# Moving a kernel's plain loads from SyncE's queue to GpSimd's, with measured durations in its planner

## The chip, the cores and the metric

The kernel runs on one core of a Trainium2 chip. The metric is device time in microseconds (us), the median over executions of the whole program. The core's engines are named as in the profile: PE is TensorE (matmuls; PEld are its weight loads), DVE is VectorE, ACT is ScalarE, POOL is GpSimd, SP is SyncE. SP computes nothing; it issues DMAs.

## What is computed

The reference takes x [2, 1024, 2048], a context [2, 2048, 2048], a weight matrix W [2048, 2048] and eight low-rank expert pairs of rank 16 with a router. Cut to what matters:

```python
def xattn(x1, x2):                       # x1: layernormed x, x2: context
    q1 = (clip(round(x1 / s1 + z1), 0, 255) - z1) * s1
    q2 = (clip(round(x2 / s2 + z2), 0, 255) - z2) * s2
    return matmul(q1, q2)                # [2,1024,2048] x [2,2048,2048]

def ffn(x):                              # x: layernormed again
    w = top2_softmax_weights(x @ W_router.T)          # 8 experts
    h = einsum('td,erd->ter', x, lora_A)
    return x @ W.T + b + 2 * einsum('ter,eor,te->to', h, lora_B, w)

x = x + xattn(layernorm(x), ctx)
x = x + ffn(layernorm(x))
```

The first matmul works on integers after rounding to 8 bits, which fp16 holds exactly. The second keeps about fp32 precision: each operand is split into a high and a low fp16 part, and three products are summed.

## The kernel before

**Work and stages.** Rows are handled in blocks of 128: eight blocks for each of the two batches (`NT`), in four pairs (`NP`). For each batch b there are these stages.

- The x blocks are loaded (`load_x`), their layernorm statistics are made on DVE (`ln1`, `stats`, `rstd_seed`), and the inverse square root is refined by a Newton chain of 16 small operations (`rstd_newton`, L389 to L400, and L582 to L584), on DVE for the very first block, on POOL for all others. ACT then quantizes to 8 bits (q, L346 through the helper `affine`), ACT or DVE shifts to fp16 (qn, L346 or L355), and a DMA transpose on SP (`transpose`, L336) makes the stationary operand `at`.
- The context is loaded in 512 KB pieces (`load_b`, tile `bs`), quantized on DVE (u, L357) and shifted to fp16 on ACT or DVE (b, L346 or L355).
- `gemm1` runs 32 units of 16 matmuls of 128x128 by 128x512 (L636). DVE adds the result into x (L657), ACT sums squares (L675). The very first matmuls are 30 warm-up ones on qn (L609).
- `ln2` makes the second layernorm's scale for a pair of blocks (POOL for three pairs, DVE for the last), and `y_prep` normalizes into yt, forms sums and differences of the row and column halves (a Strassen-like scheme of 7 products instead of 8; L749), splits each into high and low fp16 parts (nat_a, nat_s: L346 and L742) and transposes them by DMA (y_a, y_s; L336). Most halves of x are then written out to DRAM (spill) and later read back (xr, `reload`).
- `w_step` loads rows of W (wt, wb, ws), combines them on DVE (L918, L928, L932, L939, L942), scales to a high part on ACT or DVE (w, L346 or L353) and makes the low part on DVE (L902). `g2` multiplies (L1032; the low-rank part in L1046), in two column halves (`cp`) and four groups (`GROUPS`); DVE adds the result into x (L1057). `hmm` (L790, L794) makes the low-rank and router products, `router` picks two experts. `put` stores the finished blocks (L1002).
- Once only: `prep_lora` and `prep_bmax` find scales of the low-rank matrices, `w_norm` (tile wn) the norm of W. Two of these need a maximum or a sum over the partitions, which POOL makes with `partition_all_reduce` (L491, L537).

The tiles come from pools of fixed slots (48 slots of 4 KB per partition for nearly everything, tag "u"; 8 PSUM banks), so a load can start when an earlier user of its slot is done.

**What sets the order.** All work is first entered as tasks in a planner (`Plan.add`: engine, duration, buffers read and written, due time). Where a task has two engines, its durations are a dictionary and the planner picks. `Plan.rank` works due times back from the matmuls, and `Plan.order` runs a list scheduling in made-up time: each engine takes the ready task with the earliest due time that fits into the free slots; a DMA also has to find the modelled queue less than `DEPTH` = 2.5 us behind and fewer than `LANES` = 8 in flight. What comes out is one order of tasks, which is emitted as it stands. On the chip each engine runs its own part of that order, and each instruction waits for its semaphores, so the planner's times set the order but not when things happen. The lines with the durations of DMAs:

```python
add("SP", 0.47, lambda: nc.sync.dma_start(...), ..., dma=nbytes * P / 360e3)
add("SP", 1.25, lambda: nc.sync.dma_start_transpose(...), ..., dma=0.896 * cols / 1024)
```

All DMAs, that is loads, spills, transposes and stores, are issued by SP in this one order. `load` (L332) issues the loads and, with a DRAM tile as its target, the spills.

Of the kernel before, what the change touches and what calls it, by code (L numbers as in the profile page):

```python
# [11 lines left out]
F32 = mybir.dt.float32  # L12
# [5 lines left out]
ALU = mybir.AluOpType  # L18
AX = mybir.AxisListType
PSUM = bass.MemoryType.PSUM  # L20

P = 128
# [21 lines left out]
MM = 0.216  # L44
# [22 lines left out]
DMA_SLACK = 3.0  # L67

# [14 lines left out]
class Task:  # L83
    __slots__ = ("eng", "dur", "durs", "fn", "preds", "succs", "prio", "cap", "bufs", "left",
                 "ready", "start", "done", "dma", "seq", "pe", "far", "need")


class Plan:
# [3 lines left out]
    def add(self, eng, dur, fn, r=(), w=(), prio=None, cap=None, dma=None, far=None):  # L92
# [7 lines left out]
        t.far = far  # L100
# [40 lines left out]
    def order(self):  # L141
# [6 lines left out]
        dma_free = 0.0  # L148
        lag = 0.0
# [43 lines left out]
        while todo:  # L193
# [8 lines left out]
            for eng in busy:  # L202
                while busy[eng] <= now:
# [35 lines left out]
                    end = now + t.dur  # L239
                    busy[eng] = end  # L240
                    wake(end)
                    if t.dma is not None:
                        dma_free = max(now + 1.1, dma_free) + t.dma
                        t.done = dma_free + 2.0
                        lanes = [x for x in lanes if x > now] + [t.done]
                    else:
                        t.done = end + 0.2
# [22 lines left out]
def xattn_ffn_kernel(ctx, tc, x, cx, scal, wT, bias, arT, bT, out):  # L270
# [41 lines left out]
    nc.gpsimd.memset(magic, 0x5F3759DF)  # L312
    iota = const.tile([P, E], F32)
# [17 lines left out]
    def load(dst, dst_ap, src, nbytes, w, r=(), **kw):  # L331
        add("SP", 0.47, lambda: nc.sync.dma_start(dst_ap(), src() if callable(src) else src),  # L332
            r=r, w=w, dma=nbytes * P / 360e3, **kw)

    def transpose(dst, src, r, w, cols, **kw):
        add("SP", 1.25, lambda: nc.sync.dma_start_transpose(dst(), src()),  # L336
            r=r, w=w, dma=0.896 * cols / 1024, **kw)

    def affine(dst, src, n, r, w, scale=None, bias=None, only=None, **kw):
# [19 lines left out]
        durs = {"ACT": n * 0.00083 + 0.19 + 0.09 * ptrs, "DVE": n * 0.00053 + 0.08 + 0.06 * ptrs}  # L359
# [49 lines left out]
    def prep_lora(when):  # L409
        a32 = []  # L410
        ps = bank("arn")
        on = buf("u", [P, P], F32, "ones")
        add("POOL", 0.2, lambda: nc.gpsimd.memset(on.ap(), 1.0), w=[on])
        for q in range(4):
# [11 lines left out]
            def mm(q=q, s=v):  # L426
                for k in range(4):
                    nc.tensor.matmul(
                        ps.ap()[:, :AR], on.ap(), s.ap()[:, k, :], start=q + k == 0,
# [3 lines left out]
            add("PE", 1.0, mm, r=[v, on], w=[ps], prio=when + q)  # L433
# [35 lines left out]
        for q in range(2):  # L469
# [3 lines left out]
            add("DVE", 0.6,  # L473
# [4 lines left out]
    def prep_bmax():  # L478
        m = buf("sm", [P, 52], F32, "sm_bmax")
        for h in range(2):  # L480
            s = buf("u", [P, HD], F32, f"bms_{h}")
            load(s, s.ap, bT[:, h * HD : (h + 1) * HD], HD * 4, [s])
            add("DVE", 1.13,
# [6 lines left out]
        add("POOL", 1.5,  # L490
            lambda: nc.gpsimd.partition_all_reduce(  # L491
                b_max, m.ap()[:, 2:3], P, bass_isa.ReduceOp.max), r=[m], w=[bmax_b])

        def fin():
            a = m.ap()
            i = a[:, 3:4].bitcast(I32)
# [691 lines left out]
```

## Time and profile before

| | before |
|---|---|
| median of 2 runs | 966.77 us (965.12 and 968.43) |
| span of the profiled execution | 965.8 us |
| PE busy in it | 913.9 us |
| DVE, ACT, POOL busy | 734.1, 379.9, 100.0 us |
| mean granted TensorE clock | 0.989 |
| bytes moved by DMA | 243.12 MB, 252 GB/s on the mean |
| plain loads and spills (L332) | 392 |
| transposes (L336) | 75 |
| stores (L1002) | 36 |

The profiled execution is one execution of the program on the chip; its span runs from its first to its last instruction, and is 1.0 us under the median of the runs. A matmul counts as PE busy; a weight load (PEld) runs beside it. DMA-issuing instructions are not counted as busy: their rows carry the engine's name with a q (SPq), and their length is the time that the issue held that engine. In a timeline each row has start, length, engine, line, operation, out<-in, and in brackets the engine's idle time ahead of it and what ended that. In the list of waits the idle time of an engine is summed by what ended it. The granted clock (PEclk) is given in shares of full speed.

By stages: PE starts with the warm-up at 14.56 us and is full from 41 to 158 us (first matmul of batch 0); the second matmul of batch 0 runs until about 500 us, the first of batch 1 until about 614 us, the second until 962 us.

### The profile page before, as it was taken

Reading aid. Unit: us, or ns where it says so; the run is one execution under the profiler, and the core shown is the slowest. Engines: PE = TensorE matmul, PEld = TensorE weight load, DVE = VectorE, ACT = ScalarE, POOL = GpSimd, SP = SyncE. Lnnn points to the kernel's source line nnn. Section 1 sums busy time; section 2 is a strip of 40 time slices with the busy share of each in tenths; the row PEclk is TensorE's granted clock in tenths of the full one; section 3 lists DMA queues with packets and bytes.
Section 4 is the critical chain, followed back from the end, with each engine's and each line's share of the span. In section 5 each row is a group of like instructions: output and inputs, shape, how many; then the busy total and the mean of one; then the engine's idle time right before and its main releaser. Section 6 shows DMA issues by size and latency. Waiting matters only on the chain.

```text
span 965.8 us, 12426 instructions
## 1 busy us (share of the span) xinstructions
PE 913.9 (95%) x4478; PEld 431.5 (45%) x4478; DVE 734.1 (76%) x1229; ACT 379.9 (39%) x440; POOL 100.0 (10%) x353
## 2 busy tenths in 40 slices
PE   3699998997999999999999999997898999999998
PEld 1245445454444444444444444545543444444443
DVE  7579887996988876999555778987597876699231
ACT  3466785641425422243555644641230321225000
POOL 3405431000000000005220223000000000000000
PEclk9799999999999999999999999999999999999999
DMA  9999999899899986966999979899978479695011
GB/s 319 246 392 336 303 313 243 214 189 233 246 302 389 360 312 244 363 219 242 239 273 356 319 190 228 245 215 185 255 180 262 163 272 325 207 356 171 34 66 66
DMA packets 225518, 243.12 MB, mean 252 GB/s; under 512 B 160944, under 2 KB 162992, under 8 KB 225456
## 3 DMA queue, kind: packets, MB, share of 16 engines
q1 hardware_dynamic: 225456, 242.33, 83.0%
q8 instruction: 35, 0.57, 0.2%
q14 instruction: 27, 0.22, 0.1%
HBM read 172.03 MB, written 31.46 MB: 211 GB/s over the span
## 4 chain that ended last, share of the span: by engine, by line
PE 62%; DVE 19%; POOL 6%; DMA 5%; issue 5%; ACT 2%; SPq 1%; DVEq 0%; POOLq 0%; ACTq 0%
PE X L1032 28%; PE Y L1032 19%; PE g L636 11%; DVE yt_a L749 2%; DVE nat_s L742 2%; DVE w L902 2%; PE X L1046 2%; PE Y L1046 2%; DVE nat_a L742 2%; DMA wb<-in_wT_dram 2%; DVE xr L1057 1%; POOL sm L399 1%; POOL sm L395 1%; DMA wt<-in_wT_dram 1%; DVE x L657 1%
## 5 line engine op out<-in xcount | busy, mean ns | idle before, releaser
L636 PE MATMUL g<-b,at 128*128 128x512 f16 x1024 | 228.5, 386 | 9.2 <-ACT b L346 7.4
L1032 PEld LDWEIGHTS <-y_s 128*128 128x128 f16 x1536 | 149.8, 98 | 192.4 <-issue 9.9
L1032 PE MATMUL Y<-w,y_s 128*128 128x512 f16 x768 | 207.1, 380 | 5.7 <-DVE hf L809 2.8
L1032 PE MATMUL X<-w,y_s 128*128 128x512 f16 x768 | 207.7, 381 | 4.3 <-DVE w L902 2.6
L1032 PE MATMUL X<-w,y_a 128*128 128x512 f16 x768 | 190.4, 380 | 4.5 <-DVE w L902 2.6
L1032 PEld LDWEIGHTS <-y_a 128*128 128x128 f16 x1152 | 112.5, 98 | 144.9 <-issue 7.3
L636 PEld LDWEIGHTS <-at 128*128 128x128 f16 x1024 | 101.4, 99 | 133.6 <-issue 17.5
L346 ACT ACTIVATE w<-wb,gW 128x1024 f16<-128x1024 f32 x59 | 67.4, 1147 | 190.3 <-DVE wb L932 94.3
L1032 PE MATMUL Y<-w,y_a 128*128 128x512 f16 x384 | 103.3, 379 | 3.8 <-DVE xr L1057 2.7
L902 DVE SCALAR_TENSOR_TENSOR w<-wb,gW,w 128x1024 f16<-128x1024 f32 x64 | 81.6, 1278 | 11.7 <-ACT w L346 11.3
L357 DVE TENSOR_SCALAR u<-bs,rec,sc 128x1024 uint8<-128x1024 f32 x64 | 50.9, 808 | 27.5 <-DMA bs<-in_cx_dram 22.0
L346 ACT ACTIVATE b<-u,nz 128x1024 f16<-128x1024 uint8 x47 | 53.0, 1143 | 44.7 <-DVE u L357 40.2
L1057 DVE SCALAR_TENSOR_TENSOR xr<-X,uW,xr 128x512 f32<-128x512 f32 x70 | 50.5, 744 | 25.7 <-PE X L1046 23.2
L1057 DVE SCALAR_TENSOR_TENSOR xr<-Y,uW,xr 128x512 f32<-128x512 f32 x45 | 33.2, 742 | 36.0 <-PE Y L1046 36.0
L657 DVE SCALAR_TENSOR_TENSOR x<-g,s,x 128x512 f32<-128x512 f32 x64 | 47.4, 745 | 10.3 <-PE g L636 10.1
L346 ACT ACTIVATE q<-x,sm 128x1024 uint8<-128x1024 f32 x32 | 38.0, 1232 | 34.0 <-POOL sm L584 29.2
L928 DVE TENSOR_TENSOR wb<-wt 128x512 f32<-128x512 f32 x32 | 21.9, 687 | 34.4 <-DMA wt<-in_wT_dram 28.7
L939 DVE TENSOR_TENSOR wb<-wb,wt 128x1024 f32<-128x1024 f32 x32 | 38.7, 1218 | 11.5 <-DMA wb<-in_wT_dram 11.5
L742 DVE TENSOR_TENSOR nat_s<-yt_a,nat_s 128x1024 f16<-128x1024 f32 x32 | 38.3, 1217 | 5.5 <-ACT nat_s L346 5.5
L367 DVE BATCH_NORM_STATS2 sm<-x 128x6 f32<-128x512 f32 x64 | 40.4, 680 | 2.5 <-DMA x<-in_x_dram 2.4
L346 ACT ACTIVATE nat_s<-yt_a 128x1024 f16<-128x1024 f32 x27 | 27.8, 1049 | 33.3 <-DMA y_s<-nat_s 14.9
L790 PE MATMUL ph<-ar,y_a 128*128 128x272 f16 x192 | 37.0, 284 | 3.9 <-DVE xr L1057 2.1
(157 smaller groups left out, 901.8 us busy)
## 6 DMA issues: line engine op xcount, KB each, us to landing
wt<-in_wT_dram SPq DMA_DIRECT2D x88, 512.0 KB, 6.4
bs<-in_cx_dram SPq DMA_DIRECT2D x64, 512.0 KB, 9.9
wn<-in_wT_dram SPq DMA_DIRECT2D x32, 512.0 KB, 7.6
wb<-in_wT_dram SPq DMA_DIRECT2D x32, 512.0 KB, 8.1
x<-in_x_dram SPq DMA_DIRECT2D x30, 512.0 KB, 8.3
spill<-x SPq DMA_DIRECT2D x28, 512.0 KB, 4.0
xr<-spill SPq DMA_DIRECT2D x28, 512.0 KB, 6.8
out_dram<-xr SPq DMA_DIRECT2D x24, 512.0 KB, 4.2
```

What stands on the lines that cost most here:

```text
L346: nc.scalar.activation(o, i, AF.Copy if c is None else AF.Identity, scale=1.0 if a is None else a, bias=0.0 if c is None else c,)
L357: nc.vector.tensor_scalar(o, i, a, c, ALU.mult, ALU.add)
L367: nc.vector.bn_stats(st[:, 2 * h + c], b.ap()[:, c * C : (c + 1) * C])
L636: nc.tensor.matmul(ps.ap(), aT.ap()[:, k, :], S["b", c, k // 4].ap()[:, k % 4, :], start=k == 0, stop=k == KT - 1,)
L657: nc.vector.scalar_tensor_tensor(xs, ps.ap(), s12, xs, ALU.mult, ALU.add, accum_out=s.ap()[:, o : o + 1])
L742: lambda: nc.vector.tensor_tensor(n.ap()[:, 1], t.ap(), n.ap()[:, 0], ALU.subtract), r=[t], w=[n])
L790: nc.tensor.matmul(ph.ap()[:, : 2 * AR], y[half].ap()[:, 0, k, :], ar[:, kr, :], start=kk == 0, stop=False,)
L902: lambda: nc.vector.scalar_tensor_tensor(w.ap()[:, 1, lo:up], src(), g, w.ap()[:, 0, lo:up], ALU.mult, ALU.subtract),
L939: lambda: nc.vector.tensor_tensor(bot.ap(), bot.ap(), top.ap(), ALU.subtract),
L1032: nc.tensor.matmul(ps.ap(), y.ap()[:, a, k, :], w.ap()[:, q, j * C : (j + 1) * C], start=k == 0 and fresh and i == 0, stop=k == HK - 1 and ...
L1046: nc.tensor.matmul(ps.ap(), hT.ap()[:, 2 * p + tt, a], lb.ap()[:, q], start=False, stop=i == 2, skip_group_check=True,)
L1057: nc.vector.scalar_tensor_tensor(xs, ps.ap(), uW[:, cp : cp + 1], xs, ALU.mult, ALU.add)
```

## The change

Four things change, all in the way that work is issued and ordered; the arithmetic on the tensors is the same.

1. `load` issues from POOL (`nc.gpsimd.dma_start`) instead of SP. That is all 392 loads and spills of the program. Transposes and stores stay on SP.
2. The two sums over partitions leave POOL. The maximum of lora_B goes out to a DRAM tile as a column and comes back as a row to every partition, and DVE reduces it. The sum for W's norm becomes a matmul with a matrix of ones on PE, into a PSUM bank of its own; the ones, so far a buffer of `prep_lora`, are a constant made at the start.
3. The planner's durations and its model of DMAs change: a plain DMA takes 1.0 us of POOL and lands 1.9 us after its transfer at 405 KB/us; a transpose (`turn`) holds SP until everything in flight has landed, and lands 2.5 us later; most DVE durations grow by about 0.08 us; a DVE or ACT task frees its engine a little before its end (`NEXT`).
4. The quantization u of the context may go to ACT as well as to DVE (`only="DVE"` is dropped).

The diff, without the lines that only change a duration:

```diff
+RATE = 405e3
+LAND = 1.9
+TURN_LAND = 2.5
+NEXT = {"DVE": 0.08, "ACT": 0.1}
...
                     end = now + t.dur
+                    if t.dma is not None:
+                        if t.turn:
+                            end = max(end, land)
+                            dma_free = max(dma_free, end + t.dma)
+                            t.done = end + TURN_LAND
+                        else:
+                            dma_free = max(end + 0.2, dma_free) + t.dma
+                            t.done = dma_free + LAND
+                        land = max(land, t.done)
+                        lanes = [x for x in lanes if x > now] + [t.done]
+                    else:
+                        t.done = end + 0.1
+                        end -= NEXT.get(eng, 0.0)
                     busy[eng] = end
                     wake(end)
-                    if t.dma is not None:
-                        dma_free = max(now + 1.1, dma_free) + t.dma
-                        t.done = dma_free + 2.0
-                        lanes = [x for x in lanes if x > now] + [t.done]
-                    else:
-                        t.done = end + 0.2
...
+    ones = const.tile([P, P], F32)
+    nc.gpsimd.memset(ones, 1.0)
...
     def load(dst, dst_ap, src, nbytes, w, r=(), **kw):
-        add("SP", 0.47, lambda: nc.sync.dma_start(dst_ap(), src() if callable(src) else src),
-            r=r, w=w, dma=nbytes * P / 360e3, **kw)
+        add("POOL", 1.0, lambda: nc.gpsimd.dma_start(dst_ap(), src() if callable(src) else src),
+            r=r, w=w, dma=nbytes * P / RATE, **kw)

     def transpose(dst, src, r, w, cols, **kw):
-        add("SP", 1.25, lambda: nc.sync.dma_start_transpose(dst(), src()),
-            r=r, w=w, dma=0.896 * cols / 1024, **kw)
+        add("SP", 1.35 + 0.25 * cols / 1024, lambda: nc.sync.dma_start_transpose(dst(), src()),
+            r=r, w=w, dma=0.5 * cols / 1024, turn=True, **kw)
...
-        add("POOL", 1.5,
-            lambda: nc.gpsimd.partition_all_reduce(
-                b_max, m.ap()[:, 2:3], P, bass_isa.ReduceOp.max), r=[m], w=[bmax_b])
+        d = Buf("dram", lambda: dram.tile([P, 1], F32, name="bmax"))
+        row = buf("u", [P, P], F32, "bmax_row")
+        load(d, d.ap, lambda: m.ap()[:, 2:3], 4, [d], r=[m])
+        load(row, row.ap, lambda: d.ap().rearrange("p o -> o p").to_broadcast([P, P]), P * 4,
+             [row], r=[d])

         def fin():
             a = m.ap()
+            nc.vector.tensor_reduce(b_max, row.ap(), AX.X, ALU.max)
...
-        add("POOL", 1.5,
-            lambda: nc.gpsimd.partition_all_reduce(
-                acc.ap()[:, 21:22], acc.ap()[:, 20:21], P, bass_isa.ReduceOp.add), w=[acc])
+        ps = bank(f"wsum_{cp}")
+        add("PE", 0.2,
+            lambda: nc.tensor.matmul(
+                ps.ap()[:, :1], ones, acc.ap()[:, 20:21], start=True, stop=True),
+            r=[acc], w=[ps], prio=when + WN_STEP * KT)
...
-                affine(u.ap, s.ap, HD, [s], [u], scale=r2, bias=z2, only="DVE")
+                affine(u.ap, s.ap, HD, [s], [u], scale=r2, bias=z2)
...
-            add("SP", 0.47,
+            add("SP", 0.42,
                 lambda cs=cs: nc.sync.dma_start(
...
-                r=[(xb, parts)], dma=4 * (cs.stop - cs.start) * P / 360e3, prio=t + PUT)
+                r=[(xb, parts)], dma=4 * (cs.stop - cs.start) * P / RATE, prio=t + PUT)
```

The other lines raise durations, among them DVE's tensor_tensor of 1024 elements from 1.13 to 1.22 us and of 512 from 0.6 to 0.69, DVE's bn_stats pair from 1.2 to 1.3, DVE's add after the second matmul from 0.72 to 0.75. The Newton chains' 4.0 and 4.2 us on POOL stay.

## The prediction

> **What bounds the kernel now.** I read the page first, then the busy time by stretches of 25 us, then the timelines of PE, SP, POOL and DVE around the stretches where PE is not full.
>
> From the page:
> ```profile
> PE 913.9 (95%) x4478; PEld 431.5 (45%) x4478; DVE 734.1 (76%) x1229; ACT 379.9 (39%) x440; POOL 100.0 (10%) x353
> ...
> PEclk9799999999999999999999999999999999999999
> ```
> PE is the bound: 51.9 of 965.8 us are without a matmul, and only they, and stretches at half clock, can be won. The PE timeline (idle time before the instruction, and what ended it, in brackets) places them:
> ```profile
> 14.56 9.11 PE L609 MATMUL warm<-qn 128*128 128x512 f16 x30 [14.56 <-ACT qn L346]
> ...
> 31.05 6.80 PE L636 MATMUL g<-b,at 128*128 128x512 f16 x18 [3.99 <-ACT b L346]
> ...
> 231.15 2.72 PE L1032 MATMUL X<-w,y_s 128*128 128x512 f16 x6 [1.39 <-DMA y_s<-nat_s]
> ...
> 660.08 0.28 PE L790 MATMUL ph<-ar,y_a 128*128 128x272 f16 x1 [2.06 <-DVE xr L1057]
> ```
> By stretches PE lacks 14.56 us to the warm-up, 9.2 in the head (24 to 41 us), 5.0 at 160 to 175 (A), 5.4 at 218 to 243 (B), 10.0 at 636 to 693 (C), 2.7 at 730 to 741 (D), about 4 in the tail. In B and C the granted clock falls as well (0.57 over four us at 231 and at 661, some 1.7 us lost each). A to D are the places where y is normalized and transposed while PE already multiplies. There SP's queue is the thing to see:
> ```profile
> 137.70 8.55 SPq L336 DMA_TRANSPOSE y_s<-nat_s  x1
> ...
> 179.86 1.79 SPq L336 DMA_TRANSPOSE y_a<-nat_a  x1
> ...
> 220.68 10.87 SPq L336 DMA_TRANSPOSE y_s<-nat_s  x4
> 231.60 0.83 SPq L332 DMA_DIRECT2D wt<-in_wT_dram  x1
> ...
> 674.56 5.90 SPq L336 DMA_TRANSPOSE y_s<-nat_s  x2
> 680.51 0.57 SPq L332 DMA_DIRECT2D wt<-in_wT_dram  x1
> ```
> A transpose holds SP for 1.79 us with an empty queue, but for 8.55 us behind six wn loads: it ends about when they have landed. Loads behind transposes wait in turn, and DVE pays for it (its timeline):
> ```profile
> 237.20 0.69 DVE L928 TENSOR_TENSOR wb<-wt 128x512 f32<-128x512 f32 x1 [7.72 <-DMA wt<-in_wT_dram]
> ...
> 686.25 0.69 DVE L928 TENSOR_TENSOR wb<-wt 128x512 f32<-128x512 f32 x1 [7.39 <-DMA wt<-in_wT_dram]
> ```
> The head is another matter. POOL runs the Newton steps of three row blocks without a pause from 14.86 to 35.70 us, ACT's q waits for them, and b, and so PE, behind it. POOL's operations are stretched while DVE works (POOL, then DVE):
> ```profile
> 28.80 0.19 POOL L394 TENSOR_TENSOR sm<-sm 128x1 f32<-128x1 f32 x1
> 29.07 0.59 POOL L395 TENSOR_TENSOR sm<-sm 128x1 f32<-128x1 f32 x1
> ...
> 34.39 1.31 POOL L584 TENSOR_TENSOR sm<-sc,sm 128x1 f32<-128x1 f32 x1
> ```
> ```profile
> 33.46 1.53 DVE L357 TENSOR_SCALAR u<-bs,rec,sc 128x1024 uint8<-128x1024 f32 x2
> ```
> The same operation takes 0.19 us or up to 1.3 us, ending when a DVE tensor_scalar of 0.75 to 0.81 us ends. DVE's own 0.81 does not change. One Newton chain of 16 operations lasts 4.36 us undisturbed (86.71 to 91.07); three would be 13.1 us, and took 20.8.
>
> **The change, part by part.** *392 plain DMAs go from SP to POOL* (88+64+32+32+30+28+28+32+32+12+4+4+4+2 in the list of issues); SP keeps 75 transposes, 36 stores and one small load.
>
> Mid stages. SP no longer holds loads behind transposes. In B, DVE's hole of 7.72 us goes if wt, free to be issued beside the transposes, comes on time. PE's 1.39, 0.36 and 1.65 us and the half clock (1.7) hang on it or on late transposes: 5.1, of which I take 4. In C, DVE's hole of 7.39, and the 4.83 us that nat_s waits at 669 because a transposed tile frees its buffer late, are ahead of PE's stalls: 10.0 + 1.7; I take 8. In D four transposes stand before wt and wb (issued from 725.46 on): 2 of 2.7. In A, PE's 1.11 and 0.90 us wait for transposes; the other 2.62 for DVE's w, which DVE makes when it can: 2. What is late next is DVE: it is busy 25.00 of 25 us from 175 to 225, so these stretches can't shrink further. Sum: 16 us won, between 0 (the transposes wait as before) and 26.5 (all of A to D and both clock losses, 23.1 + 3.4).
>
> Between 250 and 600 us and after 741 us PE has no gap over 0.7 us; moved loads are worth nothing there, since PE covers them. If POOL became late by more than the loads' lead, that cover would go.
>
> Cost of an issue on POOL. The trace has none. From below: SP's own rows, 0.33 to 0.48 us. From above: one operation held to its longest, 1.3 us, and 0.4 behind it: 1.7. The nearest row in kind is a custom instruction on POOL, the all-reduce of b_max with 1.24; I take 1.0, between them.
>
> Head. Up to 41.3 us POOL is busy 17.8 us and would issue 22 loads: 39.8 us at 1.0. It is just full. Thirteen loads fit ahead of the first Newton chain, as on SP. The nine that SP issued between 15.9 and 35.9 now stand between or behind the chains that PE's restart hangs on: 9 us. Against that, the 64 u conversions may go to ACT (its q row of the same form: 1.23 us; DVE 0.81), and ACT idles in the head; if half go, half of the 7.7 us by which POOL was stretched goes: 3.9. Net 5 us lost; ends: 4 won (all nine behind the chains, 3.9 won) and 15 lost (nine at 1.7).
>
> POOL also gets the waits of loads and spills for free buffers (SP waited 93.5 us for DVE's w alone). Behind them stand the Newton chains of later blocks, then ACT's q and yt. PE has no gap from 41 to 158 and from 440 to 612 us, so I cost this at nothing; without that lead each held chain would cost what it is late.
>
> *No sums on POOL.* b_max by all-reduce took 1.24 us; now a DMA out, a DMA back and a reduction: two landings of 1.7 to 2.9 us (sc, a spill), two issues and 0.29 (L438), 6 to 8 us. It was done at 144.3, and its reader waits for the sum of squares, finished after 162.3: covered by 18 us. That sum becomes a matmul in PE's queue (L428's rows: 0.28 us). PE then waits for DVE's reduction there, with hmm's matmuls behind it; it needs gW next anyway. Between 0 and 3 us, taken 0.5. The memset of ones moves ahead of the first load: 0.2.
>
> *Durations in the planner* change the order alone. That has no price in the trace; I give it 0, within the ranges above.
>
> Sum: 965.8 − 16 + 5 + 0.7 = 955.5 us of span. The profiled span stands 1.0 us under the median of 966.77, so the time is 956.5; I say 956.
>
> [...]
>
> **Rivals.**
> 1. *The whole gain* (earlier loads, and ACT takes the u's). For: DVE's holes of 7.7 and 7.4 us each end on a load; the granted clock was 0.52 over 30 to 37 us and 0.51 over 40 to 47 us, so an earlier b counts double there. Against: DVE full at 175 to 225. A to D give 24, the head costs nothing: 965.8 − 24 + 0.7 + 1, and some 3 at the head's clock: 940.
> 2. *Transposes keep their wait.* If a transpose waits for every DMA in flight, not for its own queue (the new planner assumes just that), y comes no earlier. For: DMA engines are busy 0.95 to 1.05 of the time in A to C. Against: half-size transposes (1.34 us at 14.53, with loads in flight) did not wait, so it looks like room in a queue. Four us won of 16: 968.
> 3. *POOL becomes the bound*, the one on the other side. Until 175 us POOL is busy 53.5 us and would issue 88 DMAs: 141 us at 1.0, full at (175 − 53.5)/88 = 1.38 us. At 1.7 it needs 203, 28 too many, and the mid stages keep their gaps, since DVE, full there, holds the issues too: 965.8 + 28 + 0.7 + 1 = 995. For: rows held to 1.3 us; POOL's order is fixed, so a load behind a Newton chain waits. Against: most operations there take 0.19.
>
> **How the numbers follow.** Forecast 0.36 (own range 946 to 965), whole gain 0.25, kept wait 0.15, POOL bound 0.24. Two per cent, 19 us, is about what a measurement of this kernel can tell from no change. Below 947 lie nearly all of the whole gain and a little of the forecast: 0.28 faster. Above 986 lies most of the POOL case: 0.20 slower. The rest, 0.52, is the same. The range 935 to 1000 leaves out the best of the whole gain (0.06) and the worst of the POOL case (0.09).
>
> **What would show it.** Right: transposes on SP near 1.8 to 2.5 us with loads in flight; DVE's waits for wt and wb (28.7 + 11.5 + 6.2 us in the list of waits) mostly gone; PE gaps in B and C under 6 us together. Wrong: issues on POOL over 1.4 us, ACT's q waiting for POOL past 36 us and PE's restart later than 47 us (POOL case); transposes of 4 us and more beside loads (kept wait). An order by the new planner that puts w or y later at PE would make all terms wrong.

## The result and the profile after

The changed kernel takes 1090.39 us (median; 1085.57 and 1095.22) against 966.77: 1.127 times the time before, interval 1.122 to 1.133. That is slower by 124 us, and outside the predicted range. The profiled execution has a span of 1093.4 us.

From the page of the changed kernel (the second line is the granted clock in 40 slices, the last two are rows of the issues: engine, operation, out<-in, count, then busy time and mean ns, then the idle time before them and its cause):

```profile
PE 943.8 (86%) x4482; PEld 438.1 (40%) x4482; DVE 712.5 (65%) x1196; ACT 424.0 (39%) x474; POOL 315.6 (29%) x744
...
PEclk9799969779889999999999999978999899999999
...
q0 software_dynamic: 51904, 186.80, 52.8%
q1 hardware_dynamic: 159280, 55.59, 26.7%
...
L346 POOL DMA_DIRECT2D wt<-in_wT_dram x88 | 47.0, 534 | 227.2 <-DVE w L919 45.2
L346 POOL DMA_DIRECT2D bs<-in_cx_dram x64 | 47.2, 738 | 92.4 <-issue 70.7
```

The span grew by 127.6 us. PE is without a matmul for 1093.4 - 943.8 = 149.6 us, where it was 51.9. The other 29.9 us are in PE's own busy time. The records of the granted clock show half clock for 116 us, 21 before; PE was busy in 66 of them, in 18 before, and by my estimate these 48 more, at half speed, are some 24 of the 29.9. The DMAs now run in two queues: q0 with the 186.80 MB that GpSimd issues, and q1, SyncE's. A packet, below, is an entry of the trace's list of DMA packets, and a DMA lands when its completion is signalled. POOL is not full: it is busy 29% with all its issues, and an issue takes 0.53 us for wt and 0.72 for bs (medians).

SyncE's timeline shows what became of the transposes, and PE's what hangs on it:

```profile
133.16 15.27 SPq L350 DMA_TRANSPOSE at<-qn  x1
...
184.82 2.62 SPq L350 DMA_TRANSPOSE y_s<-nat_s  x1
187.61 24.13 SPq L350 DMA_TRANSPOSE y_a<-nat_a  x1
```
```profile
161.63 1.89 PE L653 MATMUL g<-b,at 128*128 128x512 f16 x4 [19.82 <-DMA at<-qn]
...
207.46 0.41 PE L807 MATMUL ph<-ar,y_s 128*128 128x272 f16 x1 [4.95 <-DMA y_s<-nat_s]
```

The transpose issued at 133.16 lands after 28.4 us, the one at 184.82 after 22.6, though nothing stands ahead of them in SyncE's queue but transposes (some 8 of the 22.6 us are a stall of both queues, see experiment 6). All transposes from issue to landing, before and then after:

```profile
DMA to landing us min/median/max: 3.3/4.9/10.6
```
```profile
DMA to landing us min/median/max: 3.6/6.2/28.7
```

Half of them still land within 6.2 us, so the loss lies in the long ones: one of 75 took over 10 us before, 14 do now. In the list of waits (total, times, longest) the transposes now hold PE and, in turn, the loads:

```profile
POOL wb L346 <- DMA y_s<-nat_s: 38.8, 5, 12.4
...
PE g L653 <- DMA at<-qn: 30.2, 6, 19.8
...
POOL wt L346 <- DMA y_s<-nat_s: 26.3, 4, 10.9
...
POOL bmax L346 <- DVE sm L685: 25.0, 1, 25.0
```

In the list of before PE has no wait for at. The loads were then SyncE's, and its list shows these waits of loads for a y_s transpose:

```profile
SPq L332 <- DMA y_s<-nat_s: 1.2, 2, 0.8
```

The first and the third line of after are a circle: GpSimd's loads wait for slots that a late transpose sets free.

### The profile page after: what moved, and what is told of

The parts are those of the page before. It is cut to its first block, busy times and chain, and to the rows that moved or that the text cites. A ratio compares the mean times of both kernels' runs of the same rounds, so it can differ in the third digit from the quotient of the medians.

```text
span 1093.4 us, 12547 instructions
## 1 busy us (share of the span) xinstructions
PE 943.8 (86%) x4482; PEld 438.1 (40%) x4482; DVE 712.5 (65%) x1196; ACT 424.0 (39%) x474; POOL 315.6 (29%) x744
## 3 DMA queue, kind: packets, MB, share of 16 engines
q0 software_dynamic: 51904, 186.80, 52.8%
## 4 chain that ended last, share of the span: by engine, by line
DMA 29%; PE 22%; issue 18%; DVE 15%; POOL 11%; ACT 3%; SPq 1%; POOLq 0%; DVEq 0%; ACTq 0%
PE X L1049 10%; PE Y L1049 8%; DMA y_s<-nat_s 7%; DMA wb<-in_wT_dram 4%; DMA y_a<-nat_a 4%; DMA wt<-in_wT_dram 3%; DMA out_dram<-xr 3%; DMA bs<-in_cx_dram 3%; DVE w L919 3%; POOL bs L346 2%; DVE xr L1074 2%; DVE wb L956 2%; DMA hT<-hh 1%; DMA bb<-in_bias_dram 1%; POOL sm L413 1%
## 5 line engine op out<-in xcount | busy, mean ns | idle before, releaser
L653 PE MATMUL g<-b,at 128*128 128x512 f16 x1024 | 234.1, 387 | 51.4 <-DMA at<-qn 30.2
L1049 PE MATMUL Y<-w,y_s 128*128 128x512 f16 x768 | 212.5, 388 | 7.9 <-DMA y_s<-nat_s 3.8
L1049 PE MATMUL X<-w,y_a 128*128 128x512 f16 x768 | 195.9, 389 | 19.1 <-DMA y_a<-nat_a 8.1
L360 ACT ACTIVATE w<-wb,gW 128x1024 f16<-128x1024 f32 x63 | 71.6, 1146 | 212.5 <-DVE wb L959 77.2
L1049 PE MATMUL Y<-w,y_a 128*128 128x512 f16 x384 | 104.8, 383 | 15.5 <-DVE xr L1074 13.6
L346 POOL DMA_DIRECT2D wt<-in_wT_dram x88 | 47.0, 534 | 227.2 <-DVE w L919 45.2
L360 ACT ACTIVATE u<-bs,sc,rec 128x1024 uint8<-128x1024 f32 x50 | 61.5, 1238 | 50.4 <-DMA bs<-in_cx_dram 43.0
L346 POOL DMA_DIRECT2D bs<-in_cx_dram x64 | 47.2, 738 | 92.4 <-issue 70.7
L674 DVE SCALAR_TENSOR_TENSOR x<-g,s,x 128x512 f32<-128x512 f32 x64 | 47.3, 745 | 35.3 <-PE g L653 35.1
L369 DVE TENSOR_SCALAR b<-u,nz 128x1024 f16<-128x1024 uint8 x43 | 32.2, 755 | 52.5 <-ACT u L360 52.4
L346 POOL DMA_DIRECT2D wb<-in_wT_dram x64 | 34.3, 537 | 98.1 <-DMA y_s<-nat_s 38.8
L956 DVE TENSOR_TENSOR wb<-wb,wt 128x1024 f32<-128x1024 f32 x32 | 38.8, 1220 | 24.2 <-DMA wb<-in_wT_dram 24.2
L807 PE MATMUL ph<-ar,y_a 128*128 128x272 f16 x192 | 39.5, 297 | 11.1 <-DMA y_a<-nat_a 11.1
```

Of the source, the lines that this page charges most:

```text
L346: add("POOL", 1.0, lambda: nc.gpsimd.dma_start(dst_ap(), src() if callable(src) else src), r=r, w=w, dma=nbytes * P / RATE, **kw)
L360: nc.scalar.activation(o, i, AF.Copy if c is None else AF.Identity, scale=1.0 if a is None else a, bias=0.0 if c is None else c,)
L369: nc.vector.tensor_scalar(o, i, c, None, ALU.add)
L653: nc.tensor.matmul(ps.ap(), aT.ap()[:, k, :], S["b", c, k // 4].ap()[:, k % 4, :], start=k == 0, stop=k == KT - 1,)
L674: nc.vector.scalar_tensor_tensor(xs, ps.ap(), s12, xs, ALU.mult, ALU.add, accum_out=s.ap()[:, o : o + 1])
L807: nc.tensor.matmul(ph.ap()[:, : 2 * AR], y[half].ap()[:, 0, k, :], ar[:, kr, :], start=kk == 0, stop=False,)
```

## Experiments

The theories in the expectations: A, that the DMA engines serve the two queues in turn, so that a transpose with its small packets starves beside loads of the other queue; B, that GpSimd's issuing (its time, its room for descriptors, its order) delays the loads; C, that the new order is at fault.

**1. The queues by themselves.** Eight stages, each with six transposes of 128x2048 fp16, twelve loads of 512 KB, or both. Here and in experiment 6 the setting of experiment 3, `dynamic_dma_scratch_size`, is 16 times the kernel's, 16384 against 1024:

```python
phase(nc.sync, False, True, False)
phase(nc.sync, False, False, True)
phase(nc.gpsimd, False, False, True)
phase(nc.sync, False, True, True)
phase(nc.gpsimd, False, True, True)
phase(nc.scalar, False, True, True)
phase(nc.scalar, True, False, True)
phase(nc.scalar, True, True, True)
```

> A kernel that computes nothing of the reference: eight stages, each with 6 transposes of 128x2048 fp16 on SP and/or 12 loads of 512 KB, with all engines joined between stages. Theory A (DMA engines take packets in turn from each queue, so a transpose's 2048 packets of 256 B, 128 on each of 16 engines, alternate with the loads' packets of 4096 B): transposes alone land about 2.5 us apart; beside loads from POOL one transpose takes some 128 x (159 + 18) ns = 23 us until the loads are through; the same beside loads that ACT issues with rows of 4 KB; beside ACT's loads with rows of 512 B only about 128 x (25 + 18) ns = 5 to 6 us. In SP's own queue, loads and transposes just add up (1.3 + 2.5 us). Theory B (POOL's own software issue is what is slow, or room in its queue): transposes slow down beside POOL's loads alone, not beside ACT's, and loads from POOL alone are slower than from SP alone. Theory C (the planner's order) says nothing here: all stages as the sum of their parts.

Transposes alone land 2.5 us apart. Issue to landing of these transposes alone, and then of the first one beside loads on GpSimd (the rows for one tile, minimum, median and maximum):

```profile
DMA to landing us min/median/max: 4.5/5.0/5.6
```
```profile
L63 SPq DMA_TRANSPOSE tr<-src x1: 1342/1342/1342, 114.5 to 114.5; - x1
...
DMA to landing us min/median/max: 22.3/22.3/22.3
```

With the loads in SyncE's own queue each transpose but the first landed some 7 us after its issue, and held SyncE 5 us (81.10 and 93.40 are two of them):

```profile
81.10 4.96 SPq L63 DMA_TRANSPOSE tr<-src  x1
...
93.40 4.98 SPq L63 DMA_TRANSPOSE tr<-src  x1
```

From its first issue to its last landing the stage took 40.8 us in one queue, 34.9 us with the loads on GpSimd and 34.5 with them on ScalarE. In the 40.8 the first transpose came 5.5 us after the first load, since it waited for the stage ahead; from there it is 35.3. So the two queues lost no time on this stage (35.3 us against 34.9 and 34.5); they changed who came first. With ScalarE's loads the first transpose took 15.5 us, so it isn't GpSimd alone. Rows of 512 B brought 6 to 13 us where 5 to 6 were expected (a packet of 512 B took 32 ns; the 25 of the expectation was an estimate that no run had shown).

**2. The order and the queue apart.** First the changed kernel's order with SyncE issuing; then the order of before with GpSimd issuing.

```diff
-        add("POOL", 1.0, lambda: nc.gpsimd.dma_start(dst_ap(), src() if callable(src) else src),
+        add("POOL", 1.0, lambda: nc.sync.dma_start(dst_ap(), src() if callable(src) else src),
```

> The changed kernel with its planner and order as they are, but the loads and spills issued by SP again, at the places that the plan gave them. Theory A (second queue starves the transposes): back near the time before, 960 to 1000 us, no transpose landing later than about 12 us. Theory B (POOL's few places and its fixed order with the Newton chains): also near before. Theory C (the new order by the new durations is itself bad): stays at 1060 to 1110.

```diff
-        add("SP", 0.47, lambda: nc.sync.dma_start(dst_ap(), src() if callable(src) else src),
+        add("SP", 0.47, lambda: nc.gpsimd.dma_start(dst_ap(), src() if callable(src) else src),
```

> The kernel before with its planner and order as they are, only the loads and spills issued by POOL at the places that the plan gave SP (sums over partitions still on POOL). Theory A: most of the loss, 1040 to 1110 us, with transposes of 15 to 30 us beside loads. Theory B: the same or worse, with POOL idle ahead of loads for room. Theory C: 955 to 985.

The first took 982.82 us (ratio to before 1.019, 1.014 to 1.023), the second 1080.74 (1.118, 1.109 to 1.126). The move of the loads thus costs 114 us in the old order and 108 in the new one, and C accounts for at most 18. In the second kernel, whose order is that of before, transposes took up to 22 us. Both A and B had expected this pair.

**3. Room for descriptors.** In the changed kernel GpSimd stands 70.7 us before loads of bs for which the profile names no releaser; the long ones end some 0.3 us after an earlier load has landed. The setting that the expectations call the room for its descriptors was doubled:

```diff
-        "TRN2", target_bir_lowering=False, num_devices=1, dynamic_dma_scratch_size=1024
+        "TRN2", target_bir_lowering=False, num_devices=1, dynamic_dma_scratch_size=2048
```

> The changed kernel with the space for the descriptors of POOL's DMAs doubled (1024 to 2048 B a partition), so that about 7 loads bs instead of 3, and 14 of the 4 KB rows instead of 7, fit in flight. Theory A: no gain or a loss, 1080 to 1130 us, since more loads lie beside each transpose. Theory B: a clear gain, 1000 to 1060, and the waits for room (bs in the head) gone. Theory C: 1085 to 1095.

It took 1073.62 us (1.112, 1.108 to 1.116), 17 less than the changed kernel in its own runs, between what A and B gave. GpSimd's wait before bs fell to 11.4 us, and up to seven bs were in flight where it had been three; of loads with rows of 4 KB at most eight, where 14 had been expected and seven were before. What the setting holds no run here shows; the run shows that it limits how many of GpSimd's loads are in flight. It is part of the loss, a small one.

**4. The other parts alone.** The changed kernel with its loads planned and issued on SyncE; the kernel before with only the sums off GpSimd; with only the planner's durations and its model of the queue; and with the sums by ones matmuls but the maximum left on GpSimd. The first and the last edit (the two others are hunks of the change as printed above):

```diff
-        add("POOL", 1.0, lambda: nc.gpsimd.dma_start(dst_ap(), src() if callable(src) else src),
+        add("SP", 0.42, lambda: nc.sync.dma_start(dst_ap(), src() if callable(src) else src),
```
```diff
-        add("POOL", 1.5,
-            lambda: nc.gpsimd.partition_all_reduce(
-                acc.ap()[:, 21:22], acc.ap()[:, 20:21], P, bass_isa.ReduceOp.add), w=[acc])
+        ps = bank(f"wsum_{cp}")
+        add("PE", 0.2,
+            lambda: nc.tensor.matmul(
+                ps.ap()[:, :1], ones, acc.ap()[:, 20:21], start=True, stop=True),
+            r=[acc], w=[ps], prio=when + WN_STEP * KT)
```

> The changed kernel with its loads planned and issued on SyncE (0.42 us each) again; what stays of the change is the planner's new durations and turn model, the sums off GpSimd and u on either engine. Theory A (the second queue is the whole loss, since the DMA engines take packets of the two queues in turn) expects this near the kernel before, 955 to 985 us: above it only by what the new order costs, below the 983 us of the run with the same order issued by SyncE but planned for GpSimd. Theory B (GpSimd's issues and their room are the loss) expects the same, so this run doesn't part A from B; it parts both from theory C (the new plan is at fault wherever its loads are issued), which expects over 1000 us.

> The kernel before with only the sums taken off GpSimd: the partition sums by a ones matmul on TensorE, and the maximum over partitions by a write to DRAM and a broadcast load, both in SyncE's queue. Theory A: within 6 us of 967 either way; the sums lie in the head, and the 0.5 and 0.2 us of the prediction is all they cost. Theory C: the round trip through DRAM stands in the queue that carries loads and transposes and waits there for DVE's maximum, as it held GpSimd's queue for 25 us in the changed kernel: 5 to 25 us more than before.

> The kernel before with only the planner's new durations and its model of transposes that take turns with loads; loads stay on SyncE at 0.42 us and the sums on GpSimd. Theory A: 960 to 980 us. Theory C puts the 16 us of the run with the changed order on SyncE here if the durations order the work worse: 975 to 990 us. If that run lost because its order had been planned for loads on GpSimd, this one is within 5 us of 967.

> The kernel before with the ones matmuls for the sum of squares, but the maximum over partitions still on GpSimd: the sums part without its trip through DRAM. The sums part alone took 9 us more than before. If its trip (the write behind SyncE's transposes, the broadcast read, DVE waiting 7.9 us for it) is the whole of that, this run is within 3 us of 967. If the matmul and its PSUM bank cost, 970 to 976 us.

| | us | ratio to before, interval |
|---|---|---|
| all but the move | 973.64 | 1.009 (1.006 to 1.011) |
| sums only | 975.73 | 1.010 (1.008 to 1.012) |
| durations only | 967.90 | 1.003 (1.001 to 1.004) |
| sums without the trip through DRAM | 966.86 | 1.000 (0.999 to 1.002) |

The measured durations are worth nothing. The sums cost 9 us, where A gave 6 at most, and all of it is the trip of the maximum through DRAM. With the sums alone the waits between 130 and 185 us show it:

```profile
PE ph L795 <- DMA y_a<-nat_a: 8.1, 3, 6.3
DVE b_max L498 <- DMA bmax_row<-bmax: 7.9, 1, 7.9
```

DVE stands 7.9 us for the row that comes back, and PE 8.1 us for transposes that stand in the same stretch of the queue. In the changed kernel the same trip was taken out:

```diff
-        load(d, d.ap, lambda: m.ap()[:, 2:3], 4, [d], r=[m])
-        load(row, row.ap, lambda: d.ap().rearrange("p o -> o p").to_broadcast([P, P]), P * 4,
-             [row], r=[d])
+        add("POOL", 1.5,
+            lambda: nc.gpsimd.partition_all_reduce(
+                b_max, m.ap()[:, 2:3], P, bass_isa.ReduceOp.max), r=[m], w=[bmax_b])
```

> The changed kernel with the maximum over partitions back on GpSimd, so that its queue does not stand 25 us for DVE's maximum and no 4-byte write goes out. Theory A: the loss is by transposes beside loads, so most stays: 1065 to 1095 us. The rival, that the in-order GpSimd queue held by this wait delays the loads and with them much of the kernel, expects under 1050 us.

1083.01 us (1.123, 1.120 to 1.126): 7 us under the changed kernel, with intervals that overlap. The 25 us for which the trip held GpSimd's queue were not what the kernel lost.

**5. Some loads on GpSimd.** The order of before, with GpSimd issuing only W loads: first 120 of the last groups and the second column half, then 72 of the second column half alone, where no transpose is issued (the condition printed is the second's).

```diff
+        q = nc.gpsimd if late[0] else nc.sync
-        add("SP", 0.47, lambda: nc.sync.dma_start(dst_ap(), src() if callable(src) else src),
+        add("SP", 0.47, lambda: q.dma_start(dst_ap(), src() if callable(src) else src),
...
+                    late[0] = cp == 1 and (b == 1 or grp <= 1)
                     w_step(S, b, cp, grp, k)
```

> The kernel before in its own order, with 128 of its 392 loads issued by GpSimd: W loads only, of the stretches in which few or no transposes are issued. Theory A (a transpose beside loads of another queue gets every second packet and so a tenth of its rate) expects no loss where there is no transpose to starve: 955 to 975 us. Theory B (GpSimd's issue, its room for descriptors or its writing of them costs time wherever it issues) expects a third of the 114 us of the run with all loads moved: 1000 us or so, and at least 980.

> The kernel before in its own order with W loads on GpSimd only in the second half of the output columns, where no transpose is issued (in the first such run 120 loads moved, some beside the transposes of 255 to 278 us and 721 to 744 us, and the kernel was 9.5 us slower). Theory A: without transposes to starve the second queue costs nothing: 964 to 971 us. Theory B: GpSimd's issues, waits for room and descriptors cost there too, in proportion to the loads moved: 975 us or more.

976.02 us (1.009, 1.006 to 1.012) and 971.40 (1.006, 1.004 to 1.008). Both lie at or just above the upper end that A gave, and some 4 us under the least that B asked for, so they lean to A without settling it. In the first, the two places where it falls behind are 250 to 340 us and 720 us, and some of its loads still meet y_s transposes there, up to 280 us and at 720 (one took 13.4 us). The second loses its 5 us between 300 and 380 us, with no transpose; a moved load costs 5/72 = 0.07 us, against 114/392 = 0.29 where all are moved.

**6. What a turn is.** One transpose beside twelve loads of each packet size, and a write of 128 single 4-byte elements in the midst of twelve loads:

```python
phase([nc.scalar], 1024)
phase([nc.scalar], 512)
phase([nc.scalar], 256)
phase([nc.scalar], 128)
phase([nc.gpsimd], 1024)
phase([nc.gpsimd], 512)
...
            if i == 6:
                nc.sync.dma_start(d4, col)
            load(nc.sync, i, 1024)
```

> Computes nothing of the reference; eight stages, each of 12 loads of 512 KB and (in all but the last) one transpose of 128x2048 fp16 issued by SyncE behind the second load. Theory A (each DMA engine takes packets of the two queues in turn, and a transpose has 128 packets of 256 B on each of 16 engines, 18 ns each) expects the transpose to take 128 x (18 ns + one packet of the loads): with loads issued by ScalarE and rows of 4 KB (159 ns) 22.7 us, of 2 KB (84 ns) 13 us, of 1 KB 7 to 9 us, of 512 B (28 ns by the 1.8 us per load of the first microbenchmark) 6 us. With loads on GpSimd 22.7 us with rows of 4 KB, and the same with rows of 2 KB, since GpSimd's queue packs them into packets of 4 KB. With loads on both GpSimd and ScalarE a turn costs 336 ns, so that the transpose would take 43 us and lands only with the last loads, after 30 us. Theory B (GpSimd's own issue and descriptors) expects long transposes in the GpSimd stages alone, and under 8 us in all of ScalarE's. A third theory, that the queues share the bytes evenly, expects 4 to 6 us in every stage with one other queue. Last stage: SyncE loads with one write of 128 elements of 4 B to DRAM in the midst: the stall seen beside the write of the maximum in the changed kernel would show as 5 us or more between two loads; without it 1.3 us.

From issue to landing the transpose took 18.9, 16.5, 11.0 and 10.6 us beside ScalarE's loads with rows of 4, 2, 1 KB and 512 B, and 17.7 and 13.0 us beside GpSimd's with rows of 4 and 2 KB. The order of sizes is A's, the figures are not: A gave 22.7, 13, 7 to 9 and 6, and with only eight loads in flight the 4 KB stage ran out of competitors. Neither B nor an even share of bytes (4 to 6 us) fits. The stage with two load queues overlapped with the one ahead of it; its transpose took 26.8 us, where A gave 43. What bears on A most closely are the packets in the traces of the two microbenchmarks and of the changed kernel, counted by the microsecond; the second number includes the 4-byte packets that end a DMA, and alone it is only these:

```
                                    packets of the transpose / of the other queue, us by us
alone (experiment 1)                734/32   835/0    745/24   881/8
beside ScalarE, 4 KB (experiment 1) 108/108  103/104  106/106  109/107
beside ScalarE, rows of 2 KB        171/173  182/181  178/179  179/177
beside ScalarE, rows of 1 KB        280/282  286/280  292/298
beside GpSimd, 4 KB (experiment 1)  107/103  105/109  103/100  103/106
changed kernel, 157 to 160 us        93/93    92/86    84/88
```

In these stretches it is one packet for one packet, for rows of 1 to 4 KB and two queues. It isn't all: in its first microsecond or two a transpose moves more (422/70 and 646/110 beside ScalarE's rows of 2 and 1 KB), beside rows of 512 B it had 653/261 and 766/205 before 418/421, and in the stage with three queues, from 214 to 217 us, the transpose moved 57, 46, 45 and 61 packets a us, GpSimd's loads 32, 31, 36 and 38, ScalarE's 29, 26, 26 and 27. Why, no run here shows. A transpose has 2048 packets of 256 B, 18 ns each, a load packets of 4 KB and 159 ns (medians in the kernel before); so a transpose that moves some 800 packets a us alone moves 100 beside loads and lasts some 20 us.

The 4-byte write landed 13.6 us after its issue; the load ahead of it landed at 254.87, the write at 259.88, the load behind it at 260.34. Two loads 5.5 us apart instead of 1.3: while it was written hardly a load packet moved (13 to 29 a us from 256 to 260 us). In the changed kernel a stall of the same kind stands at 188 to 195 us, while bmax is written (there as 16 packets of 32 B): 3/3, 3/3, 2/2, 3/3 packets a us. The two queues stay even in the stall too.

**7. Large packets for the transposes.** The queues stay as they are; each transpose is replaced by a plain copy of the same bytes (rows of 4 KB, which the loads of the kernel before move in packets of 4 KB). Base with SyncE's loads, then all loads on GpSimd, then the changed kernel:

```diff
-        add("SP", 1.25, lambda: nc.sync.dma_start_transpose(dst(), src()),
+        add("SP", 1.25, lambda: nc.sync.dma_start(
+            dst().rearrange("p a b -> p (a b)"), src()),
```

> The kernel before with each DMA transpose replaced by a plain copy of the same bytes between the same tiles, so that its packets are 4 KB and no longer 256 B (the operands come out unturned, so what is computed is not the reference; the instructions and waits of the other engines are the same). It is the base for the next two: 940 to 967 us, since a copy costs the queue half a transpose.

> The same (plain copies in the place of the transposes, so not the reference's result) with all loads issued by GpSimd. With transposes this step cost 114 us. Theory A: the loss is by small packets that take turns with large ones; a copy has large ones, so the step costs at most 30 us here (392 loads at the 0.07 us that each moved load cost where there was no transpose). Theory B (GpSimd's in-order queue, its waits for buffers and for room and its other work delay the loads): the loads stand in the same queue as before, so the step still costs 80 us or more.

> The changed kernel with plain copies in the place of its transposes (so not the reference's result). Theory A: at most 45 us above the first of these three, 30 for the moved loads and 16 for the order, where the changed kernel lies 123 us above the kernel before. Theory B: 95 us or more above it.

944.08, 998.07 and 999.67 us. With copies the move costs 54 us, with transposes 114. Neither theory had it: A allowed 30, B asked for 80. The changed kernel with copies lies 56 us above the base, where A allowed 45 and B asked for 95. So about 60 us are the transposes' packets, and 54 us are something else. (By experiment 1 loads of the same 512 KB land 1.3 us apart and transposes 2.5, so by my estimate a copy is also shorter; that is in the 60, and no run parts it from the packets' size.) With copies and loads on GpSimd PE waits for y over 2 us only twice (2.25 and 2.06 us). What stands in the list of waits instead belongs to the first matmul and ahead of it:

```profile
POOL bs L332 <- issue: 48.3, 35, 3.5
...
ACT q L347 <- POOL sm L585: 45.7, 11, 8.2
```

ACT's q waited 33.9 us for POOL in the base with copies, 29.2 in the kernel before. Three more runs take the rest apart: the copies with room doubled as in experiment 3; then only the loads of x and cx back on SyncE (`q=nc.sync` in their three calls), with transposes and with copies.

> Plain copies in the place of the transposes (not the reference's result), all loads on GpSimd, and twice the room for its descriptors. Without the room this took 998 us, 54 more than with loads on SyncE, and lost 40 of them in the first 165 us, where GpSimd's queue holds loads of x and cx for want of room (issue 48 us in 35 waits). If the room is the cause there, this takes 945 to 965 us. If it is as in the changed kernel, where the same doubling won 17 us, 975 to 988 us, and the rest is GpSimd's in-order work (the statistics of the first stage wait behind loads that wait for buffers).

> The kernel before in its own order with the true transposes; only the loads of x and cx stay on SyncE, all others (W, spills, A, B, bias) go to GpSimd. By the lag of the run with all loads moved against the kernel before, which grew by 47 us in its first 120 us and by 21 between 440 and 520 us (the stages that load x and cx) and by some 40 us beside the transposes of y, this loses the 40 alone: 1000 to 1015 us. If what counts is only how many loads are moved (294 of 392), it takes 1050 us or more.

> The same (loads of x and cx on SyncE, others on GpSimd) with plain copies in the place of the transposes (so not the reference's result). If the 40 us of the run with the transposes are those of starved small packets, they are gone here: 944 to 960 us. If a GpSimd queue held by waits is the cause in that stretch too, 975 us or more.

977.56 us; 1025.26 (1.062, 1.060 to 1.063); 967.18. The room is worth 20.5 us, the second of the two cases. With x and cx on SyncE the move costs 60 us with transposes, where I had expected some 40 (and the count of loads asked for over 83), and 23 with copies, which is neither of the two cases there: 37 us go with the transposes' packets, and 23 don't. This table shows where each loses: how many us later than its base (in brackets) DVE's instructions start, the median from the given us of the base on.

```
us of the base                        40   80  120  160  240  320  440  520  640  720  800  920
changed kernel (before)               20   28   46   70   73   91   94  114  118  120  128  128
all loads on GpSimd (before)          13   41   47   55   62   70   71   91   97  109  110  109
all but x and cx on GpSimd (before)   -1   10   15   22   32   42   42   43   48   52   55   54
all on GpSimd, copies (copies, SP)     6   27   32   39   40   45   50   58   53   53   55   53
the same, room doubled (copies, SP)    6   16   21   29   29   32   37   38   33   32   34   33
all but x and cx, copies (copies, SP) -1    7   12   19   19   22   20   20   20   20   22   20
```

With copies the lag grows by 3 to 6 us between 160 and 320 us and not at all after 520; with transposes it grows there by 15 and 18 us in the second row, by 20 and 11 in the third. Those stretches hold the transposes of y. What copies don't take away is lost between 40 and 160 us, and between 440 and 520: the first matmul of either batch. Of all kernels only the copies with loads on SyncE are faster than the kernel before, and they leave the turning out.

One piece of this can be read off. GpSimd's timeline and ACT's in the last kernel of the table, then ACT's in its base:

```profile
92.33 0.76 POOL L332 DMA_DIRECT2D a<-in_arT_dram  x1 [2.76 <-DVE sm L382]
93.11 0.27 POOL L390 TENSOR_SCALAR sm<-sm 128x1 f32<-128x1 f32 x1
```
```profile
97.44 2.37 ACT L347 ACTIVATE q<-x,sm 128x1024 uint8<-128x1024 f32 x2 [8.25 <-POOL sm L585]
```
```profile
91.12 2.37 ACT L347 ACTIVATE q<-x,sm 128x1024 uint8<-128x1024 f32 x2 [3.14 <-POOL sm L585]
```

Four loads of a stand ahead of a Newton chain (L390) in GpSimd's order. Each but the first starts some 0.3 us after the one ahead has landed (at 84.0, 88.5 and 92.0 us). The chain behind them starts at 93.11, in the base at 86.7, and ACT's q waits 8.25 us for it instead of 3.14.

## Why the prediction was wrong

**The step that failed is "Mid stages": "SP no longer holds loads behind transposes", 16 us won, with 0 as the worst end "(the transposes wait as before)".** It freed the loads and took the transposes' time as 1.79 us, that of an empty queue. What the runs showed in its place: a queue of its own keeps no load away from the transposes. Beside 4 KB rows one packet of either queue moved for one of the other (107/103 a us), and the transpose got about an eighth of the 734 to 881 packets a us that it moves alone. In one queue it held SyncE for 5 to 8.55 us behind loads and landed some 2 us later. The bound was wrong in sign: nothing in the profile excluded a loss. The place was right, since the lag grows where y is transposed. DVE's waits for wt and wb, which were to go, stood at 18.8 and 24.2 us (28.7 and 11.5 before): loads now wait for the slots that late transposes hold. Measured by the copies, the transposes' packets, with their longer time, cost about 60 of the 114 us.

**The second step is "I cost this at nothing"**, of the waits that POOL gets with the loads, because PE has no gap from 41 to 158 us. The cover was not there: with copies, where no transpose is starved, the lag with all loads on GpSimd is 6 us after the head and grows to 39 by 160 us, and by some 10 more in batch 1's first matmul. (The head's net 5 came out only so. In the changed kernel itself the lag at 40 us is already 20, and a transpose issued at 38.8 us landed after 17.0 and held PE again.) 20.5 of the 54 us are the room of experiment 3, a limit that no row of before shows and that I didn't bound. What the other 34 are is settled only in part. 23 us stay when x and cx are back on SyncE, nearly all of them between 75 and 200 us, so they don't need GpSimd to hold x and cx. The Newton chain that starts 6.4 us late behind the loads of a shows that GpSimd's fixed order has a share, while the lag goes from 7 to 12 us; how large it is in all, and whether the one order of urgency that is lost when two queues feed the same engines has the rest, was not tried.

**An issue on POOL at 1.0 us (0.33 to 1.7).** Measured 0.53, and 0.72 for bs, whose longest of 64 took 1.10. The rival "POOL becomes the bound" needed 1.38 and was right in sign only; POOL is busy 29%. ACT's q waited for POOL 46 us and not 29 with all loads moved in the old order, so "a load behind a Newton chain waits" has its reverse too. In the changed kernel, with the new order, it waited 13.4 us, so there this is not the loss.

**The kept-wait rival, 968 us.** Its sign in the profile came: transposes of 4 us and more beside loads. But these transposes didn't wait for all DMAs in flight; they ran beside them, one packet in two (93/93 in the us from 157 on in the changed kernel), and so they lost more than the wait that was to go: up to 28.7 us from issue to landing, where before no transpose took over 10.6.

**Sums: 0.5 + 0.2.** The matmuls cost nothing (966.86 us). The trip cost 9 us; I priced it as two landings "covered by 18 us" and not as what stands in a queue and stalls it. The 18 was a misreading too: DVE's L497 reads b_max at 150.26 in the kernel before, 6 us after the maximum was done, and DVE's later work stands behind it. **Durations: 0.** Measured 967.90, at most 0.4% more. The order that the new planner made for GpSimd cost 18 us on SyncE, 8 of which the kernel planned for SyncE has as well.

## What to carry to other kernels

Before a DMA is moved to another queue, look at what else will be in flight and how large its packets are. Here two queues moved one packet each (107/103 a us beside rows of 4 KB), so that a DMA of small packets (a transpose) was starved by loads from GpSimd's queue and from ScalarE's alike: 22.3 and 15.5 us from issue to landing, where those in the queue of the loads, but for the first, took some 7. In this kernel the transposes were better off in the queue of the loads, and a wait of a few us there was cheaper than two queues. What a moved load costs depends on what it meets: 0.07 us where nothing is turned, 54/392 = 0.14 over all with copies for the transposes, 0.29 with the transposes. And GpSimd, which issued loads in a fixed order with its own work, made each wait for the other: a Newton chain started 6.4 us late behind four loads of the tile a, and the write of bmax held GpSimd's queue for 25.0 us until DVE was done.

## What the runs showed of the hardware

- Of two queues one packet each, once both were well under way: 107/103 (4 KB, experiment 1), 178/179 (2 KB) and 286/280 (1 KB, both experiment 6) in a us, 93/93 in the us from 157 on and 3/3 in the stall of the changed kernel. Beside rows of 512 B it was not even (418/421 only after 653/261 and 766/205), nor with three queues (57/32/29, both experiment 6).
- While a write of 128 single 4-byte elements to DRAM was in flight (13.6 us from issue to landing in experiment 6, 12.0 in the changed kernel), the core's DMA traffic nearly stood: for about 4 us in experiment 6 (13 to 29 load packets a us; 5.5 us between two loads instead of 1.3) and for some 7 us in the changed kernel (188 to 195 us).
- In the changed kernel at most seven of GpSimd's 512 KB loads with rows of 4 KB were in flight, but three of bs with rows of 2 KB; with `dynamic_dma_scratch_size` doubled it was eight and seven (experiment 3), and the kernels won 17 (experiment 3) and 20.5 us (experiment 7).
- GpSimd's queue moved bs in packets of 4 KB (q0 has no packet of 2 KB among its 51904), where SyncE's had moved its rows of 2 KB one by one (q1 had 26112 packets of 2 KB before, 1024 after).
